# Moving the second score pass of the first four attention steps four ticks earlier

## The chip, the cores and the metric

The kernel runs on one core of one Trainium2 chip. The time is the device time of one execution in microseconds (us); for the kernel before the median of three runs is 1195.03 us (1191.51 to 1197.48). The engines are TensorE (PE in the profile, with its weight loads as PEld), VectorE (DVE), ScalarE (ACT), GpSimd (POOL) and SyncE (SP), whose queue issues nearly all transfers.

## The reference

Two sequences of 1024 tokens, 128 wide, pass through two blocks. Each part is followed by a residual and a layer norm:

1. retention with 8 heads, a group norm, a gate and an output projection;
2. causal attention with 16 heads of width 8 (keys and values from a latent of width 64), then four experts of which each token uses one;
3. full attention with 16 heads of width 8, with two score entries forced to -1e9;
4. a product with a ternary weight.

The change lies in the two attentions (parts 2 and 3). Cut to what matters, both compute:

```python
scores  = einsum('bhqd,bhkd->bhqk', q, k) * D ** -0.5     # causal mask in part 2
weights = softmax(scores, axis=-1)
out     = einsum('bhqk,bhkd->bhqd', weights, v)
```

## The kernel before

**Retention.** The retention (part 1) is computed first, in sixteen chunks of 128 tokens. Its last chunk is interleaved with the first ticks of the attention.

**Steps and items.** The attention is cut into 32 steps. A step is one attention (`a`: 0 for part 2, 1 for part 3), one sequence `b`, one block of 512 queries `k`, and one group `g` of four heads. The four heads lie in the four 32-row strips of the 128 partitions. Every step computes its scores twice.

The first pass (`score`, tile `sc`) has the queries on the partitions. VectorE takes the maximum of each row (`maxima`, L348 with the causal mask added, L353 without). When the last item of a step is done, `shifts` combines the maxima (`lowered`, L360), and one tick later `enter` transposes them on TensorE (`m_ps`, L369), copies them on ScalarE (`m_rows`, L373) and lets SP's queue store them into a spare row of the queries (L374). So the second pass gives scores that already have the row maximum taken off.

The second pass (`shifted`, tile `sct`) has the keys on the partitions. ScalarE takes the exponential (`exps`, tile `es`, L397), GpSimd zeroes what lies above the diagonal (`bar`, L405), and one tick later TensorE multiplies by the values (`product`, tile `acc`). ScalarE copies the product out of PSUM (`oT` for the first item of a step, L419, or `part`, L422) and GpSimd adds it up (L423). After the last item of a step `finish` transposes the sum (`o_ps`, L187) and VectorE divides by the row sums (`o_tok`, L430 and L431).

An item of the first pass is 128 queries against up to 512 keys; an item of the second pass is 128 keys against up to 512 queries. A causal step with `k` = 0 has four items in each pass, of widths 512, 384, 256 and 128. All other steps have eight. There are 224 items of each pass. Steps 0 to 3 have `k` = 0, so they make up the first sixteen items of each pass.

**Ticks.** The order of the work is written out by hand. `chain_tick(tick)` issues the item of the first pass with that number, and the item of the second pass that is `AHEAD` = 11 numbers behind. Two heads of one and two heads of the other are issued in turn. The product comes a tick after its second-pass item, `finish` three ticks after. Since a step of four items ends at its fourth tick, steps 0 to 3 start their second pass eight ticks after their own last maxima; a step of eight items that is eleven ticks behind starts it four ticks after.

**Side work.** Ahead of each tick `side_work` issues at most some stages of other jobs, in two lanes. The light lane holds the inputs of the second sequence (`mla_inputs`) and of the second attention, the ternary weight (`ternary`, after the transfer of the expert weights `m_w`) and the outputs. The heavy lane holds the experts. A job may begin at a tick that `ends` gives for the steps that it reads: four ticks after the last second-pass item of the block. For the first block that is tick 30. A stage of `mla_inputs` projects on TensorE (`mpr`), copies on ScalarE (`mrope`, L265), rotates on GpSimd (L267, `dense` L270) and stores (`kT<-dense`, L249). The normalised input (`xn`, L224) shares its buffer with one of the `dense` tiles; it is transposed on TensorE (`xn_ps`, L187).

**PSUM.** From the first tick on, every matmul result takes the next of the eight PSUM banks in turn (`ring_of`), so a result can be written only when the result eight places before it has been read.

Of the kernel before, what the change touches and what calls it, by code (L numbers as in the profile page):

```python
# [20 lines left out]
NG, GH, HD = 4, 4, 8  # L21
# [5 lines left out]
NH = NG * GH  # L27
VW = HD + 1
VN = (NH - 1) * VW + HW
AHEAD = 11  # L30


def _columns(*parts):
# [27 lines left out]
def block_kernel(  # L61
# [252 lines left out]
    s_items, t_items = [], []  # L314
# [8 lines left out]
    s_last = {it[0]: n for n, it in enumerate(s_items)}  # L323
    t_last = {it[0]: n for n, it in enumerate(t_items)}
    parts, lowered, es, sums, pools, o_tok = {}, {}, {}, {}, {}, []

    def score(item, heads):
        i, c, half, n = item
        a, b, k, g = steps[i]
        tok = slice(k * BT + c * P, k * BT + (c + 1) * P)  # L330
        if i not in parts:
            parts[i] = small.tile([P, NC, GH, NB], F32, tag="parts", name="parts")
        got = []
        for j in heads:
            sc = slot("sc")
            rws = hrows(j)
            mm(sc[:, :n], qT[b][rws, g, tok], kT[b][rws, g, half * BT : half * BT + n])
            got.append((j, sc))
        return got

    def maxima(item, got):
        i, c, half, n = item
        a, b, k, g = steps[i]
        for j, sc in got:
            part = parts[i][:, c, j, half : half + 1]
            if a == 0 and half == k:
                spare = early.tile([P, BT], F32, tag="spare", name="spare")
                nc.vector.tensor_tensor_reduce(  # L348
                    out=spare[:, :n], in0=sc[:, :n], in1=causal[:, BT - n :], scale=1.0,
                    scalar=-3.0e38, op0=ALU.add, op1=ALU.max, accum_out=part,  # L350
                )
            else:
                nc.vector.tensor_reduce(part, sc[:, :n], AX.X, ALU.max)  # L353

    def shifts(i):

        a, b, k, g = steps[i]
        n_half = NB if a else k + 1
        lowered[i] = small.tile([P, GH, NC], F32, tag="lowered", name="lowered")
        nc.vector.tensor_reduce(  # L360
            lowered[i].rearrange("p j c -> p c j"), parts[i][:, :, :, :n_half], AX.X, ALU.max,
            negate=True,
        )

    def enter(i):

        a, b, k, g = steps[i]
        tp = slot("m_ps")
        nc.tensor.transpose(  # L369
            tp[: GH * NC, :P], lowered[i].rearrange("p j c -> p (j c)"), ident  # L370
        )
        rows_of = small.tile([GH * NC, P], F32, tag="m_rows", name="m_rows", bufs=2)
        nc.scalar.copy(rows_of, tp[: GH * NC, :P])  # L373
        nc.sync.dma_start(out=qT[b][ONE::HW, g, block_of(k)], in_=rows_of)  # L374

    def shifted(n_item, heads):
        i, kt, lo = t_items[n_item]
        a, b, k, g = steps[i]
        n = BT - lo
        if n_item not in es:  # L380
            es[n_item] = pools["work"].tile([P, GH, BT], F32, tag="es", name="es")
        got = []
        for j in heads:
            sct = slot("sct")
            rws = hrows(j)
            mm(
                sct[:, :n], kT[b][rws, g, kt * P : (kt + 1) * P],
                qT[b][rws, g, k * BT + lo : (k + 1) * BT],
            )
            got.append((j, sct))  # L390
        return got

    def exps(n_item, got):
        i, kt, lo = t_items[n_item]
        n = BT - lo
        for j, sct in got:
            nc.scalar.activation(es[n_item][:, j, :n], sct[:, :n], AF.Exp, scale=scale)  # L397

    def bar(n_item):

        i, kt, lo = t_items[n_item]
        a, b, k, g = steps[i]
        if a == 0 and kt * P >= k * BT:
            d = es[n_item][:, :, :P]
            nc.gpsimd.affine_select(  # L405
                out=d, in_=d, pattern=[[0, GH], [1, P]], compare_op=ALU.is_ge, fill=0.0,
                base=0, channel_multiplier=-1,
            )

    def product(n_item):  # L410
        i, kt, lo = t_items[n_item]
        a, b, k, g = steps[i]
        acc = slot("acc")
        for j in range(GH):
            at = (g * GH + j) * VW
            mm(acc[hrows(j), lo:], v_aug[b][:, kt, at : at + HW], es[n_item][:, j, : BT - lo])
        if kt == 0:
            sums[i] = pools["work"].tile([P, BT], F32, tag="oT", name="oT")
            nc.scalar.copy(sums[i], acc)  # L419
        else:  # L420
            part = pools["work"].tile([P, BT], F32, tag="part", name="part", bufs=1)
            nc.scalar.copy(part[:, lo:], acc[:, lo:])  # L422
            nc.gpsimd.tensor_tensor(sums[i][:, lo:], sums[i][:, lo:], part[:, lo:], ALU.add)  # L423

    def finish(i):
        a, b, k, g = steps[i]
        tp = transposed(sums[i].rearrange("p (c t) -> p c t", c=NC), "o_ps")
        tp = tp.rearrange("p (h w) -> p h w", w=HW)
        rec = small.tile([P, NC * GH], F32, tag="rec", name="rec")
        nc.vector.reciprocal(rec, tp[:, :, ONE])  # L430
        nc.vector.tensor_tensor(  # L431
            o_tok[b][k][:, :, g * GH * HD : (g + 1) * GH * HD].rearrange(
                "p c (j d) -> p c j d", d=HD
            ),
            tp[:, :, :HD].rearrange("p (c j) d -> p c j d", c=NC),
            rec.rearrange("p (c j) -> p c j", c=NC).unsqueeze(3).to_broadcast([P, NC, GH, HD]),
            ALU.mult,
        )

    n_items = len(s_items)  # L440

    s_first = {}
    for n, it in enumerate(s_items):
        s_first.setdefault(it[0], n)

    def step_of(a, b, k, g):
        return ((a * B + b) * NB + k) * NG + g

    def ends(a, b, k):

        return t_last[step_of(a, b, k, NG - 1)] + AHEAD + 4

    def starts(a, b, k):
        return s_first[step_of(a, b, k, 0)]

    def chain_tick(tick):
        si = tick if tick < n_items else None
        ti = tick - AHEAD if 0 <= tick - AHEAD < n_items else None
        for s_heads, t_heads in (((0, 1), (2, 3)), ((2, 3), (0, 1))):
            got_s = score(s_items[si], s_heads) if si is not None else ()  # L460
            got_t = shifted(ti, t_heads) if ti is not None else ()
            if si is not None:
                maxima(s_items[si], got_s)
            if ti is not None:
                exps(ti, got_t)
        if ti is not None:
            bar(ti)
        if si is not None and s_last[s_items[si][0]] == si:
            shifts(s_items[si][0])
        ai = tick - AHEAD - 1  # L470
        if 0 <= ai < n_items:
            product(ai)
        si = tick - 1
        if 0 <= si < n_items and s_last[s_items[si][0]] == si:
            enter(s_items[si][0])
        ai = tick - AHEAD - 3
        if 0 <= ai < n_items and t_last[t_items[ai][0]] == ai:
            finish(t_items[ai][0])


    with ExitStack() as rc:
# [29 lines left out]
        at, n = R_CONST["cs"]  # L511
# [307 lines left out]
        with tc.manual_schedule():  # L819
# [46 lines left out]
            n = n_chunks - 1  # L866
# [38 lines left out]
    for i, name in enumerate(("w1", "w2")):  # L905
        at, n = M_W[name]
# [153 lines left out]
    def outputs(b, k):  # L1060

        got = {}
        yield from project(o_tok[b][k], lw["wo"], "lo", got, "joT")
        r3 = scratch("sq", "r3")
        nc.vector.tensor_tensor(flat(r3), got["py"], flat(x2[b][k]), ALU.add)
        mv, r = stats(tiles(r3))
        yield 1
        x3 = scratch("mrope", "x3")
        apply(tiles(x3), tiles(r3), mv, r)
        yield 1  # L1070
        yield from project(x3, w3, "lf", got, "joT")
        r4 = scratch("xn", "r4")
        nc.vector.tensor_tensor(flat(r4), got["py"], flat(x3), ALU.add)
        mv, r = stats(tiles(r4))
        yield 1
        ob = scratch("xnT", "ob")
        apply(tiles(ob), tiles(r4), mv, r)
        at = b * T + k * BT
        nc.sync.dma_start(out=out[at : at + BT, :].rearrange("(c p) d -> p c d", p=P), in_=ob)
        yield 1  # L1080
# [5 lines left out]
    class Job:  # L1086
# [10 lines left out]
    light = [  # L1097
        Job(0, starts(0, 1, 0), padding(1)),
        Job(12, ends(0, 0, 0), setup()),
        Job(0, starts(0, 1, 0), mla_inputs(1, 0)),  # L1100
        Job(0, starts(0, 1, 1), mla_inputs(1, 1)),
    ]
    heavy = []
    for b in range(B):
        made = [Job(ends(0, b, k), starts(1, b, 0) - 3, experts(b, k)) for k in range(NB)]
        heavy += made
        for k in range(NB):
            light.append(
                Job(ends(0, b, NB - 1), starts(1, b, 0), attn_inputs(b, k), made[k : k + 1])
            )  # L1110
    last_tick = n_items + AHEAD + 4
    light += [Job(ends(1, b, k), last_tick, outputs(b, k)) for b in range(B) for k in range(NB)]
    lanes = [heavy, light]

# [151 lines left out]
```

## Time and profile before

| | us |
|---|---|
| median of three runs | 1195.03 |
| profiled execution | 1191.54 |
| its span | 1189.8 |
| TensorE busy (matmul) | 1102.6 |
| VectorE busy | 825.9 |
| ScalarE busy | 710.4 |
| GpSimd busy | 479.8 |

The profiled execution is one run with the profiler on. Its span is the time from the first to the last instruction; the rest of its time, 1.7 us, lies around it. A busy time is a sum over the whole span; matmuls overlap, and their ends are modelled. The mean clock granted to TensorE was 0.975 of full speed. Idle time of an engine is listed with the instruction that ended it, as `<-` and that instruction's engine and tile.

### The profile page before, as it was taken

Reading aid. Unit: us, or ns where it says so; the run is one execution under the profiler, and the core shown is the slowest. Engines: PE = TensorE matmul, PEld = TensorE weight load, DVE = VectorE, ACT = ScalarE, POOL = GpSimd, SP = SyncE. Lnnn points to the kernel's source line nnn. Section 1 sums busy time; section 2 is a strip of 40 time slices with the busy share of each in tenths; the row PEclk is TensorE's granted clock in tenths of the full one; section 3 lists DMA queues with packets and bytes.
Section 4 is the critical chain, followed back from the end, with each engine's and each line's share of the span. In section 5 each row is a group of like instructions: output and inputs, shape, how many; then the busy total and the mean of one; then the engine's idle time right before and its main releaser. Section 6 shows DMA issues by size and latency. Waiting matters only on the chain.

```text
span 1189.8 us, 22189 instructions
## 1 busy us (share of the span) xinstructions
PE 1102.6 (93%) x8554; PEld 604.3 (51%) x8554; DVE 825.9 (69%) x1822; ACT 710.4 (60%) x1439; POOL 479.8 (40%) x491
## 2 busy tenths in 40 slices
PE   6999999979889999999999999999989989998993
PEld 5888888755444554554444444444333333333322
DVE  4666766757766667676666677667788888888812
ACT  2465544432666556655565557556768867886891
POOL 4466445411656434443353334423333333323342
PEclk9999999986999999999999999999999999999996
DMA  5511112101000000100010001000100000000000
GB/s 187 164 37 45 41 41 45 28 10 73 10 11 19 1 2 1 21 3 1 2 19 1 1 4 18 2 1 1 19 10 2 1 2 10 1 2 10 1 1 9
DMA packets 14840, 25.56 MB, mean 21 GB/s; under 512 B 2960, under 2 KB 8400, under 8 KB 14352
## 3 DMA queue, kind: packets, MB, share of 16 engines
q1 hardware_dynamic: 14080, 22.30, 7.7%
q8 instruction: 67, 1.10, 0.4%
q0 software_dynamic: 224, 1.05, 0.2%
q10 hardware_dynamic: 432, 0.81, 0.2%
q14 instruction: 37, 0.30, 0.1%
HBM read 10.13 MB, written 1.05 MB: 9 GB/s over the span
## 4 chain that ended last, share of the span: by engine, by line
PE 72%; DVE 17%; POOL 4%; issue 3%; ACT 2%; DMA 1%; SPq 0%; POOLq 0%; DVEq 0%; ACTq 0%
PE sc L82 17%; PE acc L82 15%; PE sct L82 12%; PE pmoe L82 5%; PE ph L82 5%; DVE parts L353 5%; DVE spare L348 2%; PE py L82 2%; PE pv L82 2%; PE pr L82 2%; PE pout L714 1%; PE o_ps L187 1%; PE pg L82 1%; DVE x L205 1%; ACT es L397 1%
## 5 line engine op out<-in xcount | busy, mean ns | idle before, releaser
L397 ACT ACTIVATE es<-sct 128x512 f32<-128x512 f32 (+3 forms) x896 | 426.9, 558 | 218.6 <-PE sct L82 169.0
L353 DVE TENSOR_REDUCE parts<-sc 128x1 f32<-128x512 f32 x640 | 396.9, 682 | 94.4 <-PE sct L82 69.0
L82 PE MATMUL sc<-kT,qT 32*128 32x512 f32 (+3 forms) x1792 | 428.4, 584 | 5.5 <-DVE parts L348 2.7
L82 PE MATMUL sct<-qT,kT 32*128 32x512 f32 (+3 forms) x1792 | 410.6, 578 | 1.4 <-DMA qT<-m_rows 1.1
L423 POOL TENSOR_TENSOR oT<-oT,part 128x512 f32<-128x512 f32 (+3 forms) x192 | 217.5, 1133 | 392.3 <-ACT part L422 388.0
L82 PE MATMUL acc<-es,v_aug 128*32 128x512 f32 (+3 forms) x1792 | 221.6, 558 | 40.6 <-DVE parts L353 29.0
L82 PEld LDWEIGHTS sc<-kT,qT 32*128 32x128 f32 x1792 | 171.7, 189 | 145.2 <-DVE parts L353 73.9
L82 PEld LDWEIGHTS sct<-qT,kT 32*128 32x128 f32 x1792 | 179.1, 184 | 46.0 <-issue 23.3
L348 DVE CUSTOM_DVE_ANT_0 spare<-sc,causal 128x512 f32<-128x512 f32 (+3 forms) x256 | 125.4, 490 | 48.2 <-PE sc L82 12.8
L82 PEld LDWEIGHTS acc<-es,v_aug 128*32 128x32 f32 x1792 | 37.8, 108 | 196.0 <-DVE parts L353 112.5
L422 ACT COPY part<-acc 128x512 f32<-128x512 f32 (+3 forms) x192 | 105.7, 550 | 42.4 <-PE acc L82 36.3
L405 POOL TENSOR_SCALAR_AFFINE_SELECT es<-es 128x512 f32<-128x512 f32 x64 | 40.8, 637 | 118.5 <-ACT es L397 118.5
L771 ACT ACTIVATE og<-pt,cols_sb 128x128 f32<-128x128 f32 x128 | 46.5, 468 | 53.1 <-PE pt L763 53.1
L82 PEld LDWEIGHTS pmoe<-m_w,hT 128*128 128x128 f32 x512 | 59.6, 192 | 16.2 <-DVE parts L353 8.8
L82 PE MATMUL pmoe<-m_w,hT 128*128 128x128 f32 x512 | 65.0, 280 | 0.6 <-DVE parts L348 0.2
L82 PE MATMUL ph<-xnT,m_w 128*128 128x512 f32 x128 | 62.4, 610 | 0.0
L118 POOL TENSOR_TENSOR rstd<-rstd,nhalf 128x4 f32<-128x4 f32 (+1 forms) x44 | 54.7, 1244 | 3.6
L970 DVE TENSOR_SCALAR hT<-ph,cols_sb 128x512 f32<-128x512 f32 x32 | 24.0, 750 | 35.2 <-PE ph L82 35.2
L645 POOL TENSOR_TENSOR swap<-swap,r_cs 128x1024 f32<-128x1024 f32 x16 | 38.7, 2417 | 20.7 <-DMA swap<-plain 20.7
L982 DVE SCALAR_TENSOR_TENSOR moe_acc<-pmoe,oh,moe_acc 128x128 f32<-128x128 f32 x64 | 22.4, 350 | 35.2 <-PE pmoe L82 34.8
L668 ACT COPY v<-pv 128x1024 f32<-128x1024 f32 x16 | 16.2, 1012 | 43.8 <-PE pv L82 43.8
L82 PEld LDWEIGHTS ph<-xnT,m_w 128*128 128x128 f32 x128 | 21.7, 189 | 31.0 <-issue 11.0
(178 smaller groups left out, 1190.1 us busy)
## 6 DMA issues: line engine op xcount, KB each, us to landing
swap<-plain SPq DMA_DIRECT2D x64, 128.0 KB
qT<-dense SPq DMA_DIRECT2D x32, 64.0 KB
kT<-dense SPq DMA_DIRECT2D x32, 64.0 KB
m_w<-in_m_w SPq DMA_DIRECT2D x2, 1024.0 KB
x<-in_x SPq DMA_DIRECT2D x4, 256.0 KB
mcs<-in_m_const SPq DMA_DIRECT2D x4, 256.0 KB
out<-ob SPq DMA_DIRECT2D x4, 256.0 KB
r_rest<-in_r_const POOLq DMA_DIRECT2D x1, 774.0 KB, 7.4
```

Source lines behind the costliest of these rows:

```text
L82: nc.tensor.matmul(o, lhsT, rhs, start=start, stop=stop)
L118: nc.gpsimd.tensor_tensor(r, r, nhalf[:, :n], ALU.pow)
L348: nc.vector.tensor_tensor_reduce(out=spare[:, :n], in0=sc[:, :n], in1=causal[:, BT - n :], scale=1.0, scalar=-3.0e38, op0=ALU.add, op1=ALU ...
L353: nc.vector.tensor_reduce(part, sc[:, :n], AX.X, ALU.max)
L397: nc.scalar.activation(es[n_item][:, j, :n], sct[:, :n], AF.Exp, scale=scale)
L405: nc.gpsimd.affine_select(out=d, in_=d, pattern=[[0, GH], [1, P]], compare_op=ALU.is_ge, fill=0.0, base=0, channel_multiplier=-1,)
L422: nc.scalar.copy(part[:, lo:], acc[:, lo:])
L423: nc.gpsimd.tensor_tensor(sums[i][:, lo:], sums[i][:, lo:], part[:, lo:], ALU.add)
L645: nc.gpsimd.tensor_tensor(swap[n], swap[n], table(n, 1), ALU.mult)
L771: nc.scalar.activation(og[:, a, g, :], pt[a][:, g, :], AF.Identity, bias=col("gn_b", h), scale=col("gn_w", h))
L970: nc.vector.tensor_scalar(hT[:, f, :], ph, bias, 0.0, ALU.add, ALU.max)
L982: nc.vector.scalar_tensor_tensor(acc[:, c, :], py[:, :P], oh[:, c, e : e + 1], acc[:, c, :], ALU.mult, ALU.add)
```

## The change

The item of the second pass is no longer found by a fixed distance of eleven. A list `t_tick` gives each item its tick: four ticks (`AFTER`) after the tick of its own step's last first-pass item, or one tick after the item before it, whichever is later. `t_at` is the inverse. With the steps above, the sixteen items of steps 0 to 3 come at ticks 7 to 22 instead of 11 to 26; ticks 23 to 26 have none; the first item of step 4 comes at tick 27, as before, and so does every later one. The products and `finish` of steps 0 to 3, and the tick at which the first expert job may begin (26 instead of 30), move with them.

```diff
-AHEAD = 11
+AFTER = 4
...
+    t_tick = []
+    for n, it in enumerate(t_items):
+        t_tick.append(max(s_last[it[0]] + AFTER, t_tick[-1] + 1 if n else 0))
+    t_at = {t: n for n, t in enumerate(t_tick)}
...
     def ends(a, b, k):
 
-        return t_last[step_of(a, b, k, NG - 1)] + AHEAD + 4
+        return t_tick[t_last[step_of(a, b, k, NG - 1)]] + 4
...
     def chain_tick(tick):
         si = tick if tick < n_items else None
-        ti = tick - AHEAD if 0 <= tick - AHEAD < n_items else None
+        ti = t_at.get(tick)
...
-        ai = tick - AHEAD - 1
-        if 0 <= ai < n_items:
+        ai = t_at.get(tick - 1)
+        if ai is not None:
             product(ai)
...
-        ai = tick - AHEAD - 3
-        if 0 <= ai < n_items and t_last[t_items[ai][0]] == ai:
+        ai = t_at.get(tick - 3)
+        if ai is not None and t_last[t_items[ai][0]] == ai:
             finish(t_items[ai][0])
...
-    last_tick = n_items + AHEAD + 4
+    last_tick = t_tick[-1] + 5
```

## The prediction

> **What bounds the kernel now.** I read the page first: the slices of the span, then the chain that ended last.
>
> ```profile
> PE   6999999979889999999999999999989989998993
> PEclk9999999986999999999999999999999999999996
> PE 72%; DVE 17%; POOL 4%; issue 3%; ACT 2%; DMA 1%; SPq 0%; POOLq 0%; DVEq 0%; ACTq 0%
> ```
>
> TensorE carries 72% of the chain, so over most of the span its work is the time. The exception is slices 8 to 10 (238 to 327 us): its granted clock falls to 0.8 and 0.6, and its busy share is lower on either side. The change moves work exactly there. A tick is recognised in the time line of TensorE by the width of its `sc`: the first `sct` (tick 11) starts at 284.34, tick 23 at 329.44, tick 27 at 343.18. On VectorE the maxima of tick 4 start at 268.92, of tick 7 at 277.19, of tick 11 at 287.44. So I asked for the busy time of each engine in the stages between; the columns are the stretch, its length, then TensorE, weight loads, VectorE, ScalarE, GpSimd, and the granted clock.
>
> ```profile
> core 0: us, PE busy (x) PEld busy (x) DVE busy (x) ACT busy (x) POOL busy (x), PEclk, DMA share, GB/s
> ...
> 277.20:287.40 10.20, 10.20 (x37) 6.01 (x34) 8.05 (x33) 2.38 (x4) 0.00 (x0) 0.50 0.55 206
> 287.40:299.90 12.50, 11.83 (x87) 6.71 (x85) 9.35 (x41) 6.97 (x19) 4.68 (x7) 0.85 0.01 3
> ...
> 329.44:343.18 13.74, 11.33 (x107) 6.21 (x106) 9.97 (x24) 8.04 (x22) 10.27 (x12) 1.00 0.11 21
> 343.18:360.40 17.22, 16.31 (x125) 8.27 (x124) 10.94 (x38) 12.78 (x26) 7.55 (x9) 1.00 0.03 11
> ```
>
> First row shown: ticks 7 to 10, score matmuls only. TensorE reads fully busy, but at half clock; VectorE's time line has its maxima one behind the other with gaps of about 0.2 us, so VectorE sets this pace, 10.25 us for four ticks. Second row: the first ticks with both kinds of matmul, in which the clock comes back. Third row: ticks 23 to 26, with both kinds and side work. The chain says what sets that one.
>
> ```profile
> 269.65 9.52 PE sc L82 x26
> 279.48 4.94 PE sc L82 x20
> 284.42 2.20 PE sct L82 x4
> ...
> 327.79 1.73 PE mpr L82 x4
> 330.20 2.37 POOL mrope L267
> 332.64 0.25 POOL dense L270
> 336.06 4.03 DMA kT<-dense
> 340.34 1.04 POOL xn L224
> 341.38 0.60 POOL es L405
> 342.02 0.64 PE acc L82 x8
> 342.66 0.59 PE xn_ps L187 x4
> 343.25 0.63 PE sc L82 x2
> ```
>
> From 327.8 to 343.2 the end is set by a job of the side work: two projections, rotated by GpSimd, stored by DMA. Only when that store has landed may GpSimd write the normalised block `xn` (its buffer is the one stored), and TensorE transposes it (`xn_ps`) just ahead of tick 27.
>
> **What the Trainium skill says.** "TensorE: Matmul & The Clock Gate", Part 1: TensorE runs at half clock by default and after an idle window of about 3.4 us, at full clock after a busy one, and the windows run freely. The trace agrees in size: the half-clock stretch, 267.2 to 291.1 us when the trace is asked in pieces of 3.41 us, is seven such pieces long, and ended two windows after the first `sct`. The same page, Part 3: matmuls of 32 rows in different row groups run together. In the tail four 512-wide `sct` heads take 1.07 us (1135.87 to 1136.94), where 0.59 is the length of one. "DMA: Bandwidth & Descriptors", Anatomy of one DMA: about 2 us of fixed cost, as an estimate for the rows of maxima; here their first two bursts of data are over 1.5 to 1.8 us after the issue (267.73 to 269.5; 293.70 to 295.5), so the trace's is used.
>
> **The change part by part.** Nothing is added or removed. Sixteen items of shifted scores (steps 0 to 3) move from ticks 11-26 to 7-22; from tick 27 on all stands where it stood, since step 4 is at four ticks after its maxima in both. The widths per step are 512, 384, 256, 128, a period of four ticks, so ticks 11 to 22 keep the same pairs of widths. In effect ticks 7-10 gain one step and ticks 23-26 lose one. With it `finish` of step 3 moves from tick 29 to 25, and the first expert job begins at tick 26, not 30.
>
> Size of what moves: `sct` 1280/512 x 1.07 = 2.7 us, `acc` 1.07 + 0.85 + 0.64 + 0.43 = 3.0 us, together 5.7 us of TensorE at full clock; on ScalarE 5.9 us of exponentials (2.06 + 1.74 + 1.21 + 0.88) and 1.7 of copies; on GpSimd four selects of 0.64 and three adds (1.00, 0.73, 0.46).
>
> *Ticks 7-10 gain them.* ScalarE and GpSimd are idle there (ScalarE waits 11.81 and 5.37 us), so these cost nothing; without that cover they would be the 7.6 and 4.8 us just listed. TensorE at half clock is late: tick 11 of before took 284.34 to 288.65, 4.3 us, and VectorE then sat idle 1.13 us ahead of tick 12. This start now happens at ticks 7 and 8 instead of 11 and 12: the same 1.1 us is lost once, earlier. Ticks 11 to 15 then run as 13 to 15 did, at full clock with VectorE never waiting longer than 0.3 us. Net 0; bounds -1.1 (TensorE's lead hides it) and +1.7 (the clock rises one window later).
>
> *Rows of maxima.* `enter` leaves three ticks ahead of the first reader (about 7.7 us at VectorE's pace), against 1.8 us of transfer. Nothing else stands ahead on SP's queue for steps 0 and 1; the 2 MB of expert weights issue behind step 1's rows and are over by 288, ahead of step 2's at 293.7. Cost 0, at most 1.1 each for three steps (the longest wait for these rows in the trace).
>
> *Ticks 23-26 lose them.* By engines the four ticks could shrink from 13.74 to about 10.6 us (VectorE: 9.97 plus its gaps). But the chain of the side job is not touched: projections, GpSimd, store, `xn` at 340.34 + 1.04 = 341.38. Only the select (0.60) and the product (0.64) between `xn` and its transpose go: tick 27 starts 1.24 us earlier, near 342.0.
>
> *From tick 27.* Into the idle time ahead of 342 also move what TensorE did later: the last product 0.43, `o_ps` of step 3 0.66, the wait for `o_tok` 0.83 with `moT_ps` 0.63, and `mo_ps` 1.09 (359.33 to 360.42). TensorE was 16.3 of 17.2 us busy there (last row), so these count: 3.64. Gross gain 1.24 + 3.64 = 4.9 us.
>
> *Charges.* (a) With so little in ticks 24-26, TensorE idles around 335 to 341 and the clock may fall again. One window at half clock under full work costs 3.41 / 2 = 1.7 us, two cost 3.4; the trace shows no threshold (windows with about 2 us of work stayed at full clock at 318 and fell at 254), so even odds of one to two windows: 1.3. Bounds 0 and 3.4. (b) The expert job's norm meets the rotation of the other job on GpSimd around tick 29, and the add of each product queues behind up to 3.6 us of rotation, with the next copy out of PSUM behind that: 0.6, bounds 0 and 2. Later stages move four ticks under a chain whose pattern repeats every four: 0.
>
> Sum: -4.9 + 1.3 + 0.6 = -3.0 us. The profiled execution took 1191.54 (span 1189.8), so 1188.5; against the median 1195.03 it is 1192.0. The three runs of before span 6 us, twice the effect.
>
> **Rivals.** *Fast:* the store does not hold tick 27 (its data land sooner, so `xn` is ready by 339), and ticks 23-26 run at VectorE's 10.6: 13.74 - 10.6 + 3.64 = 6.8, 1188. For it: TensorE carries 72% of the chain; against: the 4.03 us of `kT<-dense` in the chain. *Given back:* all of (a) and (b), and the clock's rise a window late, 3.4 + 2 + 0.4 = 5.8 against 4.9: 1196. *Slower:* the clock stays at half under the mixed ticks. A 512-wide mixed tick takes 3.0 us at full clock (2.0 and 1.0), so 6.0 at half, against VectorE's 3.13: each further window of 3.41 us costs about 1.6 us. Three windows eat the gain; seven (as long as the stretch before) give 7 x 1.6 - 4.9 = +6.3, 1201. For it: the trace held half clock for seven windows with score matmuls alone; against: mixed work raised it after two, and it stayed up for 877 us. *The change does nothing:* steps 4 to 31 are untouched, which is true of all but 16 of 224 items; contained in the forecast.
>
> **How the numbers follow.** About 0.5% (6 us) is what a measurement of this kernel can tell from no change. Forecast 0.48 (0.05 of it beyond -6), fast 0.20 (0.18 beyond), given back 0.17 (all within), slower 0.15 (0.13 beyond +6). So faster 0.23, same 0.64, slower 0.13. Range 1186 to 1200: the forecast and the case given back whole, most of the fast one and little of the slow one, some 0.8. The forecast's own range is 1188 to 1195.
>
> **What would show it.** The first `sct` near 274 us; full clock about 10 us earlier; VectorE's tick 16 still near 302.6; no `acc` between ticks 24 and 27; TensorE idle ahead of `xn_ps` until about 341.4, with `xn` behind `kT<-dense` in the chain; the clock in 335 to 346. Wrong it would be if tick 16 came over 2 us earlier or later, if tick 27 came before 340, or if half clock reappeared for more than two windows.

## The result and the profile after

The changed kernel takes 1198.25 us (median of 18 runs, 1195.78 to 1208.07), against 1194.86 us (18 runs) of the kernel before on the same chip: a ratio of 1.0046, with a 95% interval of 1.0026 to 1.0066. It is slower by 5.5 us (0.0046 x 1195), where 3.0 us less was forecast. (The ratio goes by all runs, whose means are 5.5 us apart; the two medians alone are 3.4 us apart.) The profiled execution took 1198.56 us, its span 1196.9.

The page of the kernel after, its slices of the span and the chain that ended last by engine:

```profile
PE   6999999979988999999999999999989989998993
PEclk8999999977989998999999999999999999999996
PE 72%; DVE 17%; POOL 5%; issue 3%; ACT 2%; DMA 1%; SPq 0%; POOLq 0%; DVEq 0%; ACTq 0%
```

By the shares nothing has happened. The digits of the clock show more. The two slices from 239 to 299 us read 7 and 7 where they read 8 and 6 before, and the twelfth (329 to 359 us) and the sixteenth (449 to 479 us) read 8 where they read 9: the clock falls in two places where it did not. A slice is 30 us long, so the stages have to be read by ticks. Below are, of the kernel after, the stages that answer to those shown of before: ticks 23 to 26, 27 to 30, 31 to 34 and 49 to 52. Columns as before: stretch, length, busy time of TensorE, weight loads, VectorE, ScalarE, GpSimd, granted clock, DMA.

```profile
332.71:348.16 15.45, 10.45 (x63) 5.75 (x62) 10.08 (x25) 1.70 (x4) 7.27 (x7) 0.78 0.09 18
348.16:362.73 14.57, 14.57 (x106) 6.43 (x105) 11.66 (x40) 11.45 (x22) 7.17 (x8) 1.00 0.01 2
362.73:387.72 24.99, 21.23 (x147) 11.19 (x146) 15.48 (x33) 12.84 (x29) 16.78 (x16) 1.00 0.10 22
453.23:469.27 16.04, 13.74 (x99) 6.42 (x98) 11.15 (x47) 8.29 (x22) 6.26 (x9) 0.79 0.01 2
```

And two of these stages of the kernel before, which its part of the text does not show (31 to 34 and 49 to 52):

```profile
360.42:377.26 16.84, 14.94 (x118) 7.20 (x118) 11.18 (x27) 10.25 (x25) 13.67 (x14) 1.00 0.07 11
444.62:459.91 15.29, 15.24 (x134) 9.07 (x134) 9.86 (x36) 7.75 (x20) 5.85 (x8) 1.00 0.01 2
```

Set side by side, with the starts of each tick's first `sc` on TensorE as bounds, the two profiled executions differ like this (us):

| stage | before | after | difference |
|---|---|---|---|
| up to tick 7 (the same program) | 272.67 | 274.90 | +2.23 |
| ticks 7 to 22 | 56.77 | 57.81 | +1.04 |
| 23 to 26 | 13.74 | 15.45 | +1.71 |
| 27 to 30 | 17.24 | 14.56 | -2.68 |
| 31 to 34 | 16.84 | 24.99 | +8.15 |
| 35 to 48 | 67.36 | 65.51 | -1.85 |
| 49 to 56 | 30.10 | 29.24 | -0.86 |
| 57 to 222 | 658.07 | 658.09 | +0.02 |
| from tick 223 | 57.04 | 56.28 | -0.76 |
| span | 1189.84 | 1196.85 | +7.01 |

The first row is not the change's: nothing differs ahead of tick 7, and in the profiled executions of kernels that add nothing ahead of it tick 7 starts anywhere from 272.3 to 279.1 us. What the change did lies in ticks 7 to 56: +5.5 us, by chance the same as the difference that the ratio gives.

Two lines matter. Ticks 23 to 26 grew, where they were to shrink by 1.24 us. Ticks 31 to 34, for which nothing was forecast, grew by half. The chain of the kernel after, in order of time, says how the first came about (start, length, what):

```profile
335.90 0.07 POOL dense L270
335.97 1.16 issue
337.13 0.45 POOL oT L423
337.58 1.01 POOL sq L218
338.59 0.02 issue
338.61 0.69 DVE ss L221
339.30 2.39 DVE parts L353 x4
341.69 0.18 DVE rec L430
341.86 0.02 issue
341.88 0.30 DVE o_tok L431
342.19 0.04 issue
342.23 1.12 PE moT_ps L187 x4
343.35 2.02 PE sc L82 x8
345.37 2.01 PE mo_ps L82 x8
347.37 0.85 PE xn_ps L187 x4
```

The store of `kT` is not in it, and `xn` is not. The transpose `moT_ps` of the expert job now stands ahead of tick 26's scores on TensorE. It needs `o_tok`; that waits on VectorE behind the four maxima of tick 25, and these behind `ss`, which waits for GpSimd's `sq`, itself behind the rotation and the last add. In the time line of TensorE (start, length, instruction, and in brackets the idle time ahead with what ended it):

```profile
342.23 1.12 PE L187 MATMUL moT_ps<-ident,o_tok 128*128 128x128 f32 x4 [4.27 <-DVE o_tok L431]
343.28 2.09 PE L82 MATMUL sc<-kT,qT 32*128 32x512 f32 x8
345.30 2.08 PE L82 MATMUL mo_ps<-m_wo,moT 128*128 128x128 f32 x8
...
365.57 1.71 PE L82 MATMUL sct<-qT,kT 32*128 32x512 f32 x4 [1.48 <-ACT part L422]
```

TensorE is idle for 4.27 us, and the clock falls at 341.3 and stays at half for two windows (in these traces half clock inside the kernel begins and ends on a grid of 3.413 us, 460.8 - 341.3 in the kernel after being 35 such pieces; one is called a window here): `mo_ps` takes 2.08 us where it took 1.16 before. So these instructions were late and then slow. The last line belongs to ticks 31 to 34; the clock falls once more at 460.8, again for 6.8 us. Neither fall is in the trace of before.

### The profile page after: what moved, and what is told of

It is laid out like the page before. It is cut to its first block, busy times and chain, and to the rows that moved or that the text cites. A ratio compares the mean times of both kernels' runs of the same rounds, so it can differ in the third digit from the quotient of the medians.

```text
span 1196.9 us, 22191 instructions
## 1 busy us (share of the span) xinstructions
PE 1106.2 (92%) x8554; PEld 602.9 (50%) x8554; DVE 828.2 (69%) x1822; ACT 711.0 (59%) x1439; POOL 479.2 (40%) x491
## 4 chain that ended last, share of the span: by engine, by line
PE 72%; DVE 17%; POOL 5%; issue 3%; ACT 2%; DMA 1%; SPq 0%; POOLq 0%; DVEq 0%; ACTq 0%
PE sc L82 17%; PE acc L82 15%; PE sct L82 13%; PE pmoe L82 5%; PE ph L82 5%; DVE parts L353 5%; DVE spare L348 2%; PE pv L82 2%; PE pr L82 2%; PE py L82 2%; PE o_ps L187 1%; PE pout L720 1%; ACT es L397 1%; DVE x L205 1%; DVE st L127 1%
## 5 line engine op out<-in xcount | busy, mean ns | idle before, releaser
L82 PEld LDWEIGHTS sc<-kT,qT 32*128 32x128 f32 x1792 | 168.5, 189 | 145.4 <-DVE parts L353 73.2
L82 PE MATMUL pv<-r_wv,xT 128*128 128x512 f32 x64 | 32.3, 629 | 5.8 <-issue 5.0
```

The lines of the kernel that those rows point to most:

```text
L82: nc.tensor.matmul(o, lhsT, rhs, start=start, stop=stop)
```

## The experiments

Every ratio is the kernel's time over that of the kernel before, measured beside it on the same chip, with its 95% interval. A thousandth is 1.2 us.

### Where the expert job begins

The first suspect was the tick at which the first expert job may begin, which the change moves from 30 to 26. In the changed kernel it can be set apart from the shifted scores:

```diff
-        made = [Job(ends(0, b, k), starts(1, b, 0) - 3, experts(b, k)) for k in range(NB)]
+        made = [Job(max(30, ends(0, b, k)), starts(1, b, 0) - 3, experts(b, k)) for k in range(NB)]
```

with 30 here, 27 and 38 in two further runs, and 34 in the kernel before.

> The changed kernel with one thing put back: the first expert job begins at tick 30 as before, not at 26. Theory A (the earlier expert job is the loss: its transpose waits for o_tok in a tick with nothing else, and its norm meets the rotation on GpSimd): below the kernel before, 1191 to 1194 us, since then 1.2 us less before tick 27 and 1.1 us of product and o_ps remain as gain and nothing is lost. Theory B (the moved second pass itself is the loss: half clock at ticks 7 and 8 and a clock that falls in ticks 23 to 26): 1197 to 1199 us, as with the whole change.

> The changed kernel with the first expert job one tick later, at 27, so that its transpose stands behind the scores of tick 26 and in front of those of tick 27. If the 4.3 us wait for o_tok ahead of tick 26 and the half clock after it are the larger part of the loss: 3 us or more below the whole change, 1194 to 1195 us. If the meeting of the expert norm with the rotation at ticks 29 to 34 is the larger part, most of the loss stays: 1196 to 1200 us. Theory B: 1198 us.

> The kernel before with only the first expert job moved, four ticks later (34, not 30). Theory A in its general form (the place of the expert job against the causal ticks 48 to 61, where VectorE sets the pace, counts by itself): 2 to 5 us below before, 1190 to 1193 us, because four stages leave ticks that TensorE sets and enter ticks 55 to 58, which VectorE sets. If only the wait and the meeting at ticks 26 to 34 count, the place makes no difference: 1193 to 1196 us. Theory B says the same, 1195 us.

> The changed kernel with the first expert job at 38, so that it ends at tick 62, just when the second one may begin, and lies over all of the causal ticks 48 to 61. Theory A in its general form: the fastest of these, 1186 to 1191 us. If the place makes no difference beyond the wait and the meeting: as with the job at 30, 1191 to 1194 us. Theory B: 1197 to 1199 us.

| kernel | median | ratio | interval |
|---|---|---|---|
| changed, job at 26 (as it is) | 1198.25 | 1.0046 | 1.0026-1.0066 |
| changed, job at 27 | 1196.12 | 1.0016 | 1.0006-1.0027 |
| changed, job at 30 | 1197.54 | 1.0029 | 1.0018-1.0040 |
| changed, job at 38 | 1191.01 | 0.9966 | 0.9954-0.9979 |
| before, job at 34 | 1197.0 | 1.0037 | 1.0021-1.0053 |

With the job back at 30 the number is theory B's: the shifted scores alone still cost 0.29%. That the job at 26 adds to it is not shown by these two ratios, whose intervals overlap. The stages do show it: with the job at 30 ticks 31 to 34 take 17.30 us, with the job at 26 24.99, and 16.84 before. Nor is later simply better: 34 in the kernel before is slower than its 30, which no theory had, and 38 in the changed one is faster than both kernels, at the border of what the two forms of theory A had. In the trace of the job at 30, the wait that the prediction named is there, in the midst of half clock:

```profile
345.18 1.11 PE L187 MATMUL xn_ps<-ident,xn 128*128 128x128 f32 x4 [3.26 <-POOL xn L224]
346.22 1.22 PE L82 MATMUL sc<-kT,qT 32*128 32x512 f32 x2
...
347.24 1.06 PE L82 MATMUL sc<-kT,qT 32*128 32x512 f32 x2
```

Ticks 23 to 26 take 13.04 us there, 0.7 less than before, and then tick 27 runs at half clock and takes 5.39 us instead of 3.54. The clock is at half from 341.1 for 10.2 us, three windows. The wait did not bring it down: it begins at 341.92 (345.18 - 3.26), after the fall. The window ahead of the fall has score matmuls and a transpose, 2.18 us of work in all, and no gap over 0.92 us:

```profile
337.64:341.05 3.41, 2.18 (x11) 0.73 (x9) 2.27 (x5) 0.00 (x0) 2.52 (x5) 1.00 0.22 58
```

With the job at 27, `moT_ps` no longer stands ahead of tick 26 (13.05 us for ticks 23 to 26), but over half of the growth of ticks 31 to 34 remains (21.80 us), and the time is at the near end of what was expected if the meeting on GpSimd is the larger part. In the kernel before with its job at 34, ticks 35 to 48 take 5.3 us less and ticks 49 to 63 9.8 us more; at 38 in the changed kernel these are 12.1 less and 13.5 more, with ticks 28 to 34 shorter by 3.6 besides. In both traces the clock also falls near 485 us, for two windows and for one. Why the sum differs so was not followed further.

### Holding the clock

To see whether half clock is the cost, TensorE was given something to do. In the kernel with the job at 30, extra matmuls of 128x512 whose result nothing reads (the filler) stand behind the score matmuls of ticks 24, 25 and 26 (in a second run also of ticks 4 to 6, where the clock falls for the first time):

```diff
+    FILL = {24: 1, 25: 1, 26: 3}
+
+    def fill(n):
+        spare_bank = slot("fill")
+        for _ in range(n):
+            mm(spare_bank, ident, causal)
...
         if ti is not None:
             bar(ti)
+        if tick in FILL:
+            fill(FILL[tick])
```

> The changed kernel with its first expert job at tick 30 (as in the earlier run), and with five extra 128x512 matmuls on TensorE, one behind the heads of tick 24, one behind those of tick 25 and three behind those of tick 26. They add work whose result nothing reads, about 0.95 us each at full clock, into time in which TensorE waits for the rotation and the store of the side job. Theory H, the half clock that comes back at 341 us is what eats the gain of ticks 24 to 28: the clock stays full there, ticks 27 and 28 fall from 5.39 us together to 3.0 to 3.5, and the time lies 2 to 3 us under that of the job at tick 30, at 1194.5 to 1195.5. Theory K, the clock has no part in it and the matmuls only add work: 1197.5 or more.

> As the kernel with five extra matmuls in ticks 24 to 26, with two more in each of ticks 4, 5 and 6, where TensorE has score matmuls only and its clock falls to half before the mixed ticks begin (again work whose result nothing reads). Theory H, the +1.0 us of ticks 7 to 23 is the mixed ticks 7 and 8 run at half clock: the clock is back before tick 7, ticks 7 to 13 take 19.8 us or less instead of 20.9, and the time is about 1 us under that of the other kernel, 1193.5 to 1194.5. Theory K, the extra matmuls delay the scores themselves: ticks 4 to 7 grow by 1 us or more and the time is 1 to 4 us over the other kernel's.

Measured: 0.9991 (0.9974 to 1.0007) with the first set, 0.9995 (0.9981 to 1.0009) with both. By the ratios, five matmuls that compute nothing of use took 0.38% away, 4.5 us (0.0038 x 1193). The two ratios come from two chips, and their intervals would allow 1.3 us as well (1.0018 to 1.0007). The trace shows where, in TensorE's time line with the first set:

```profile
339.87 2.84 PE L82 MATMUL fill<-causal,ident 128*128 128x512 f32 x6
342.96 0.66 PE L187 MATMUL xn_ps<-ident,xn 128*128 128x128 f32 x4 [0.25 <-POOL xn L224]
343.54 0.70 PE L82 MATMUL sc<-kT,qT 32*128 32x512 f32 x2
```

(A matmul in this precision counts as two in the trace, so x6 are three.) The wait for `xn` is 0.25 us instead of 3.26, the transpose takes 0.66 instead of 1.11, and there is no half clock from 283 us to the tail of the kernel (1166 us). Ticks 23 to 27 take 15.53 us (12.57 and 2.96), against 18.43 with the job at 30 alone and 17.28 before (the 5.39 us of the expectation are tick 27 by itself, which is 2.96 now). Theory H holds, and the price is 2.9 us in this stage by the trace. Each filled tick also takes one of the eight PSUM banks, which shifts the banks of all that follows; ticks 28 to 56 take the same time with and without it (59.70 and 59.68 us for ticks 28 to 34 and 49 to 56 together, 67.38 for those between), so that is not what counts. The second set did what it was to do in ticks 7 to 12 (16.09 us, where most runs have 20.9) and cost nearly the same in ticks 4 to 6 (12.66 instead of 8.24), where TensorE has too little idle time for it: what both theories had is seen in the stages, and nothing is left of it in the ratio. (In its trace the clock also falls at 621.3 us for two windows, far from the edit, and ticks 57 to 222 take 3.2 us more.)

The same was asked of the kernel before, with its first expert job at 38, without and with two extra matmuls in each of ticks 4 to 10:

> The kernel before, with only the first expert job put at tick 38 instead of 30, as in the changed kernel with that job at 38 (1191.0 us). Theory P, the place of the job is what made that one fast, and the moved shifted scores by themselves cost about 3 us of half clock: 1187 to 1189. Theory Q, the moved shifted scores are worth nothing either way: 1190 to 1192, the same as the changed kernel with the job at 38. Theory R, the gain at 38 belongs to the two edits together: about 1194.7 or more.

> The kernel before with the job at 38, and two extra 128x512 matmuls in each of ticks 4 to 10, in which the kernel before has score matmuls alone and half clock (14 matmuls, work whose result nothing reads). Theory H, half clock in ticks 4 to 12 costs about 1 to 2 us (the first mixed ticks 11 and 12 start at half clock): 1 to 2 us under the kernel with the job at 38 alone, with the clock full throughout. Theory K, VectorE sets the pace of ticks 7 to 10 whatever the clock, and the extra matmuls stand ahead of scores: the same as that kernel or up to 2 us over it.

Measured: 0.9973 (0.9962 to 0.9985) and 0.9981 (0.9972 to 0.9991). Theory Q: with the job at 38 the ratio shows no difference between the two placings of the shifted scores, 0.9966 against 0.9973. The filler in ticks 4 to 10 gives nothing here either, as theory K had it.

If half clock is what eats the shifted scores' gain with the job at 38 too, holding the clock at full must bring it out. And with the job at 26 as the change has it, the same filler tells whether the place costs only through the clock. The edits are those above (with one, three and one matmuls in the second case, since the wait lies between ticks 25 and 26):

> The changed kernel with the job at tick 38 and the extra matmuls, one, one and three, behind the heads of ticks 24, 25 and 26 (work whose result nothing reads). With the job at 38 the two placings of the shifted scores took the same time (ratios 0.9966 and 0.9973). Theory H, that is because the clock falls again at 339 us and eats what the four ticks gain: with it held full, ticks 23 to 28 fall from 17.2 to about 15.5 us and the ratio to 0.994 to 0.9955. Theory Q, the moved items are worth nothing even so: 0.9960 to 0.9975.

> The changed kernel as it is, its first expert job at tick 26, with five extra 128x512 matmuls, one behind the heads of tick 24, three behind those of tick 25 and one behind those of tick 26 (work whose result nothing reads), so that TensorE has work while it waits for o_tok. Against the kernel before the changed kernel stood at 1.0046, the one with its job at 30 at 1.0029, and that with the job at 30 and the extra matmuls at 0.9991. Theory L, the clock and the place of the job are two separate losses: the clock stays full at 341, ticks 23 to 28 take 15.5 to 16.5 us instead of 18.4, but ticks 31 to 35 still take about 25 us, and the ratio is 1.001 to 1.002. Theory M, the place costs only through the clock: 0.999, as with the job at 30.

The job at 38 with filler: 0.9961 (0.9945 to 0.9977). Ticks 23 to 27 fall from 17.19 to 15.54 us, as theory H had it, with no half clock from 282 us to the tail; but the ratio lies in theory Q's range, next to H's, and its interval holds the 0.9966 without filler, so the gain is seen in the stage and not proved in the whole.

The job at 26 with filler: 1.0056 (1.0036 to 1.0077), no better than without. That was neither theory. The clock stays full at 341, and ticks 23 to 27 fall from 18.41 to 16.59 us; then it falls at 365.9 for three windows, and ticks 31 to 34 take 28.4 us instead of 25.0. In TensorE's time line:

```profile
364.54 1.95 PE L82 MATMUL sct<-qT,kT 32*128 32x512 f32 x4 [1.48 <-ACT part L422]
366.42 1.94 PE L82 MATMUL acc<-es,v_aug 128*32 128x512 f32 x8
368.29 1.87 PE L82 MATMUL pgate<-m_gate,xnT 128*128 128x4 f32 x8
```

It falls behind the second wait. In the profiled execution of the changed kernel as it is, no fall followed the same wait; here, and in the run with filler in ticks 49 to 51 below, one did. The Trainium skill, "TensorE: Matmul & The Clock Gate", Part 1, has the windows run freely, and the traces fit that. Here the wait (363.06 to 364.54) lies inside the one window that ends with the fall, and in the run with filler in ticks 49 to 51 too (365.63 to 367.11, window 365.09 to 368.50); TensorE is busy for 1.93 us in both windows. In the changed kernel as it is, the wait (364.09 to 365.57) lies across a window's end, counted in steps of 3.413 us from the fall at 341.33, and TensorE was busy for 2.28 us in the window that holds most of it:

```profile
361.81:365.22 3.41, 2.28 (x20) 1.12 (x16) 3.33 (x7) 0.81 (x3) 3.01 (x3) 1.00 0.03 14
```

So the same wait cost 1.7 us there (next run) and 5.2 here (with the 3.45 added). Falls that come and go from one execution to the next would also give two kinds of times, and the 18 of the changed kernel lie in two groups, ten from 1195.8 to 1198.6 and eight from 1201.1 to 1208.1. The mean granted clock of the second group is lower, 0.961 to 0.967 against 0.971 to 0.975: an estimate from the groups' means, 0.008 x 1200 us, doubled, is some 20 us more at half clock, more than this one fall. But of the second group there is no trace, so where it lies is not known.

### The wait for the copy

That wait is a chain on two engines. ScalarE's copy of a shifted product out of PSUM goes to a buffer `part`, of which there is one, and must wait until GpSimd has added the one before. In the kernel after, GpSimd works from 356 to 363.6 us at the expert job's norm and at the side job's norm, rotation and `dense`, with the add behind them. In ScalarE's time line of the kernel after, and of the changed kernel with two such buffers:

```profile
364.93 0.59 ACT L422 COPY part<-acc 128x512 f32<-128x512 f32 x1 [2.60 <-POOL oT L423]
365.41 0.69 ACT L228 ACTIVATE xnT<-xn_ps,cols_sb 128x512 f32<-128x512 f32 x1
366.00 2.06 ACT L397 ACTIVATE es<-sct 128x512 f32<-128x512 f32 x4
```

```profile
363.30 0.59 ACT L422 COPY part<-acc 128x512 f32<-128x512 f32 x1
363.81 0.69 ACT L228 ACTIVATE xnT<-xn_ps,cols_sb 128x512 f32<-128x512 f32 x1
364.93 2.06 ACT L397 ACTIVATE es<-sct 128x512 f32<-128x512 f32 x4 [0.44 <-PE sct L82]
```

```diff
-            part = pools["work"].tile([P, BT], F32, tag="part", name="part", bufs=1)
+            part = pools["work"].tile([P, BT], F32, tag="part", name="part", bufs=2)
```

> The changed kernel with two buffers for the copy that takes a shifted product out of PSUM, instead of one, so that the next copy no longer waits for GpSimd's add of the one before it. Theory L, in ticks 31 to 35 the norm of the expert job, the rotation and the add stand one behind the other on GpSimd, and TensorE's sct waits for that copy: its 1.5 us wait near 365 goes, ticks 31 to 35 fall from 25.0 to 23 to 24 us, and the ratio from 1.0046 to 1.003 to 1.004. Theory N, that stage is longer only by the 6.9 us of expert matmuls that moved into it: no change there, 1.0040 to 1.0050.

Measured: 1.0029 (1.0013 to 1.0046). The 2.60 us in front of the copy are gone, and ticks 31 to 34 take 23.28 us instead of 24.99: theory L in the stage, for 1.7 us of the 8.15. The ratio's interval overlaps that of the changed kernel without the second buffer, so the whole time alone would not show it.

### What is left of the place

Four more runs asked for the rest. In the changed kernel the expert job also ends four ticks earlier, at tick 49, and the clock falls there at 460.8.

> The changed kernel with extra 128x512 matmuls behind the heads of ticks 49 (one), 50 (two) and 51 (two), work whose result nothing reads, where its expert job has already ended (it ends four ticks earlier than before) and the clock falls for 6.8 us at 460.8. Theory G, the time that the earlier job gives back at its end is lost to half clock: the clock stays full there, ticks 49 to 53 fall from 16.0 us to 11 to 13, and the ratio from 1.0046 to 1.001 to 1.003. Theory N, VectorE sets the pace of these ticks and the clock does not matter, the extra matmuls only fill: 16 us as before and 1.004 to 1.006.

> The changed kernel, its expert job at tick 26 as it stands, with the extra matmuls in ticks 24 to 26 (one, three, one) and 49 to 51 (one, two, two), work whose result nothing reads, and two buffers for the copy of the shifted product. Alone, the first of these moved the fall of the clock from 341 to 366 us, where TensorE waits for that copy (1.0056), and the second took the wait away (1.0029). Theory G, the three losses are half clock and the wait for the copy, and the place of the job costs nothing beyond them: no half clock after 290 us, ticks 23 to 28 at 16.6 us, 31 to 35 at 23 to 23.5, 49 to 53 at 11 to 13, and the ratio 0.997 to 0.999. Theory P, an earlier job costs in itself, in TensorE's work between ticks 31 and 35 that nothing gives back: 1.001 to 1.004.

> The changed kernel, its expert job at tick 26 as it stands, with the extra matmuls of ticks 24 to 26 (one, three, one; work whose result nothing reads) and two buffers for the copy of the shifted product, nothing in ticks 49 to 51. With five extra matmuls there besides it took 1.0019 of the time before. Theory G, at full clock in ticks 24 to 36 the earlier job costs only what half clock near 460 us takes from its end: 23 to 28 at 16.6 us, 31 to 35 at 23.3, the fall at 458 to 461 us is there, and the ratio is 0.999 to 1.001. Theory P, the place costs beyond both stalls and the extra matmuls of ticks 49 to 51 were paid for by the clock they held: 1.0015 to 1.003.

> As the run without extra matmuls in ticks 49 to 51, with two matmuls in tick 50 whose PSUM bank is taken ahead of the tick's scores, so that they can run in the 1.1 us in which TensorE waits for VectorE's maxima there (work whose result nothing reads, about 2 us). Theory G, the half clock of 6.8 us near 460 does not come, ticks 49 to 53 fall from about 15.5 us to 12.5 to 13.5, and the time is 2 to 3 us under that run's. Theory N, VectorE holds these ticks: it has 11 us of work there, the norm of the expert job among it, and the time is the same or 1 us more.

| changed kernel, job at 26, with | ratio | interval | 23-27 | 31-34 | 49-52 |
|---|---|---|---|---|---|
| nothing | 1.0046 | 1.0026-1.0066 | 18.41 | 24.99 | 16.04 |
| filler 24-26 | 1.0056 | 1.0036-1.0077 | 16.59 | 28.44 | 15.16 |
| two `part` buffers | 1.0029 | 1.0013-1.0046 | 18.40 | 23.28 | 15.21 |
| both | 1.0007 | 0.9994-1.0020 | 16.59 | 23.28 | 16.07 |
| filler 49-51 | 1.0049 | 1.0033-1.0064 | 17.90 | 28.39 | 17.02 |
| both, filler 49-51 | 1.0019 | 1.0008-1.0029 | 16.59 | 23.29 | 17.49 |
| both, two matmuls in 50 | 1.0034 | 1.0021-1.0048 | 16.58 | 23.28 | 16.74 |

Filler and second buffer together bring 1.0056 and 1.0029 to 1.0007, in theory G's range, with an interval that reaches into theory P's. The two stalls are 3.9 thousandths, 4.7 us, of the 5.5; by the stages of the traces 3.5 us (207.57 and 204.04 us for ticks 7 to 56). They are not additive: the filler alone brings nothing, and in its trace the second stall costs a fall of the clock besides.

Ticks 49 to 52 gave no answer of that kind. The clock was held there in one run of three (with filler alone), and the filler cost what it saved, or more; the 11 to 13.5 us that theory G had for these ticks never came, and the ratios are those of theory N (filler 49-51 alone) and theory P (with both stalls away). VectorE has 11.15 us of work in these ticks, the expert job's closing norm among it, and TensorE's spare time of 2.3 us (16.04 - 13.74) is too small for five matmuls of about 1 us. The 1.0034 of the last row cannot be laid to tick 50 alone: in its trace the clock also falls at 622.6 for two windows, and ticks 57 to 222 take 3.0 us more than without these matmuls. So that half clock near 460 us takes anything is not shown. What the stages do show: with both stalls away, ticks 31 to 34 are still 6.44 us longer than before (23.28 - 16.84), and only 2.7 us come back in ticks 35 to 56 (1.84 + 0.86). In ticks 31 to 34 stand 8 `pgate`, 8 `ph` and 16 `pmoe` instructions more of the trace, and in ticks 35 to 56 as many fewer. Here are ticks 31 to 34 with both stalls away, and below them those of the run with the job at 30 and the same number of filler matmuls:

```profile
365.10:388.38 23.28, 20.20 (x148) 10.96 (x147) 15.54 (x33) 12.56 (x29) 16.79 (x16) 1.00 0.11 24
```

```profile
358.92:376.10 17.18, 14.94 (x118) 7.22 (x117) 11.54 (x27) 10.48 (x26) 13.69 (x14) 1.00 0.08 17
```

TensorE is busy for 5.26 us more, which is most of the 6.10 that the stage is longer. In ticks 49 to 52 before, TensorE was busy 15.24 of 15.29 us; in the kernel after it is busy 13.74 of 16.04, so there the time is no longer its own. What holds these ticks instead was not taken apart.

The last run puts together what helped, with the job at 38:

> The changed kernel with the job at tick 38, the extra matmuls in ticks 24 to 26 (one, one, three; work whose result nothing reads) and two buffers for the copy of the shifted product. Without the second buffer it took 0.9961 of the time before. Theory L, the wait for that copy is a part of the time wherever rotation and adds meet on GpSimd: 0.994 to 0.9955. Theory N, it matters only where the expert job's norm meets them in ticks 31 to 35, which the job at 38 avoids: 0.9955 to 0.997.

Measured: 0.9942 (0.9920 to 0.9964; 5 runs). It is the fastest of all by its ratio, 7 us under the kernel before, though its interval overlaps that with one buffer (0.9961). Ticks 31 to 34 take 16.35 us against 16.15 there, so the second buffer did nothing at the place it was to act on. The ratio is theory L's, but no stage of its trace is shorter than without the buffer, so whether it helps elsewhere is not settled. That the job at 38 with the filler beats both kernels is.

## Why the prediction was wrong

**Ticks 7 to 10 gaining the step: net 0, bounds -1.1 and +1.7.** In size right. Ticks 7 to 22 take 56.77, 57.37 and 57.48 us in three executions without the moved items, and 57.8 to 59.0 in thirteen with them and no filler ahead of tick 7: +0.4 between the middle ones. The first `sct` was at 276.31, and tick 7 started 2.2 us later than before for reasons ahead of the change, so near 274 as said, and the clock came back at 283.3, ten us earlier counted from tick 7. VectorE's tick 16 came 3.3 us late, 1.1 without these 2.2: within the 2 us.

**Rows of maxima: 0.** Nothing in the traces speaks against it.

**Ticks 23 to 26: tick 27 starts 1.24 us earlier, held by `xn`.** Right only with the job at 30 and the clock held at full: there these ticks take 12.57 us, 13.74 less 1.17, and `xn` releases tick 27 as told. In the changed kernel itself the step failed. The working put `moT_ps` "into the idle time ahead of 342" together with its wait for `o_tok`, as if the wait were over by then. It wasn't: `o_tok` was ready at 342.17, and `moT_ps` stood ahead of tick 26's scores. With the clock held this wait costs 1.06 us (13.63 against 12.57). What was missed is an order: a stage of side work goes ahead of a tick's scores, so what it waits for is paid by the scores behind it. The 0.83 us that the trace of before shows for this wait belonged to another place.

**From tick 27: -3.64.** Measured -2.68. Of the 0.96 that is missing, 0.65 is the `xn_ps` of the expert job, which moves into these ticks from the following ones and which the sum didn't count.

**Charge (a), the clock falls again in ticks 24 to 26: +1.3.** That the clock may fall there was right, and the size too small. It fell there in every profiled execution of the changed kernel in which nothing filled these ticks, with the job at 26, 27, 30 or 38, for two windows or three. Held, ticks 23 to 27 are 1.8 us shorter with the job at 26 and 2.9 with it at 30. The 1.3 is half the cost of one to two windows, even odds that the clock falls at all; it should have been near certain. A window cost less than the 1.7 put for it, 0.9 to 1.0 (an estimate, 1.8 / 2 and 2.9 / 3), for TensorE waits in a part of it. In the kernel after it is the idle time "around 335 to 341", as the prediction had placed it: the window ahead of the fall had 0.12 us of TensorE work. With the job at 30 that window had 2.18 us, so a long gap is not needed.

**Charge (b), expert norm and rotation meet on GpSimd: +0.6, bounds 0 and 2.** The mechanism was right, down to the copy out of PSUM queued behind the add. It measured 1.7 us in the stage, and 5.2 where the clock fell behind it.

**"Later stages move four ticks under a chain whose pattern repeats every four: 0".** This is the step that failed most. The chain's pattern repeats, but what TensorE has beside it doesn't. The four ticks that the expert job gains (31 to 34) hold the side job's projections and GpSimd's work already and grow by 6.4 us without the copy's wait; those that it leaves (49 to 56) are held by other things and shrink by 0.9, ticks 35 to 48 by 1.9. That is +3.7 where 0 was put. With the job back at 30 and the rest of the change in place, these stages take 17.30 (31 to 34), 67.38 (35 to 48) and 30.09 us (49 to 56), against 16.84, 67.36 and 30.10 before: it is the place of the job that moves them. The ratios alone do not tell: with filler, the job at 26 stands at 1.0007 with the copy's wait away, and the job at 30 at 0.9991 with the wait never there, but the intervals overlap. So the cost is shown in the stages, and not in the whole time.

Put together from the trace, the forecast of 0 - 4.9 + 1.3 + 0.6 + 0 = -3.0 reads, for ticks 7 to 56, +1.0 - 2.8 + 1.8 + 1.7 + 3.7 = +5.4 (5.5 unrounded), where -2.8 is ticks 23 to 30 with the clock held (28.2 us from the run with filler, against 30.98), against the 5.5 of the table. These are sums over single executions; the +1.0 is 0.4 between the middle ones. Of the rivals, "given back" (1196) came nearest: it took all of (a) and (b). "Slower" by half clock under mixed ticks did happen (10.2 us of it ahead of and in tick 27 with the job at 30), but ended after three windows; "fast" is excluded, since with the clock held `xn` still kept tick 27, or `o_tok` tick 26. The range of 1186 to 1200 held the time; the direction was wrong.

## What to carry to other kernels

Work that was taken out of a stage whose end something else holds hardly shortened it (13.04 us instead of 13.74); it left TensorE idle, and what followed paid for the idle time a second time, at half clock (5.39 us instead of 3.54). When a job's earliest start moves, cost it where it goes to and where it leaves, from the windows of both stages: here the stage that it entered paid 6.4 us, and those that it left gave back 2.7. And of a stage that is to run ahead of other work, ask first when its operand is ready.

## What was not expected of the hardware

The Trainium skill, "TensorE: Matmul & The Clock Gate", section "Why this matters for your kernels", advises no idle gaps of TensorE over about 3 us. The wait of 4.27 us with a fall at 341.3 agrees. But the traces go further: shorter gaps do it too, as in the window of the job at 30 shown above. The rows below are more windows ahead of a fall, of the kernel after (two of them), of the run with the job at 26 and filler, and of the run with two matmuls in tick 50; each was followed at once by half clock:

```profile
337.84:341.25 3.41, 0.12 (x1) 0.00 (x0) 2.64 (x5) 0.00 (x0) 1.95 (x3) 1.00 0.33 73
457.41:460.80 3.39, 2.04 (x28) 1.08 (x24) 3.10 (x11) 1.45 (x5) 2.21 (x3) 1.00 0.00 0
```

```profile
362.50:365.90 3.40, 1.92 (x10) 0.78 (x6) 2.93 (x12) 2.00 (x4) 2.63 (x3) 1.00 0.20 56
```

```profile
451.90:455.30 3.40, 2.60 (x21) 1.52 (x19) 3.11 (x12) 1.48 (x5) 2.18 (x3) 1.00 0.00 0
```

TensorE was busy 0.12, 2.04, 1.92 and 2.60 of 3.4 us in them; in the last three no gap was longer than 1.5 us. Against that, a window of the kernel before with 2.09 us stayed at full clock:

```profile
318.42:321.83 3.41, 2.09 (x26) 0.72 (x21) 3.00 (x10) 1.59 (x4) 2.79 (x4) 1.00 0.09 33
```

So the busy time of a window doesn't decide by itself; what the throttle counts isn't known from these traces. That five matmuls which nobody reads can buy time (2.9 us in the stage; 1.0029 to 0.9991 in the ratio) was not expected either, nor that such matmuls, where TensorE has too little idle time to take them, cost what they save (ticks 4 to 6: 4.4 us more, ticks 7 to 12: 4.8 less).
